# Selective scan with two states of a half in one scan instruction, and softplus from ScalarE's logarithm

## The chip, the cores and the metric

The kernel runs on one core of one Trainium2 chip. The metric is the device time of one execution in microseconds (us), taken as the median of several runs. The engines are named as the profile names them: PE is TensorE's matmul (PEld its weight load), DVE is VectorE, ACT is ScalarE, POOL is GpSimd, and SP is the engine that issues the plain DMAs. [...]

## What is computed

One layer adds two branches to its input. `x` is (2, 2048, 256) and is layer-normalized first. All data is float32.

```python
xn = _layernorm(x)
x  = x + attn(xn) + ffn(xn)

# attn: tokens sorted by the nearest of 8 means, then a Mamba scan along the sorted row
x_dbl = einsum('bdl,cd->bcl', u, x_proj_weight)          # u = sorted xn, transposed: (2, 256, 2048)
dts, Bm, Cm = x_dbl[:, :32], x_dbl[:, 32:48], x_dbl[:, 48:] + prompt
delta = softplus(einsum('brl,dr->bdl', dts, dt_projs_weight) + dt_projs_bias)
A = -exp(A_logs)                                           # (256, 16)
def step(h, (u_t, d_t, b_t, c_t)):                         # h: (2, 256, 16), along 2048 steps
    h = exp(d_t[..., None] * A) * h + (d_t * u_t)[..., None] * b_t[:, None, :]
    return h, einsum('bdn,bn->bd', h, c_t)
y = scan(step) + Ds * u                                    # then back to the old token order

# ffn: top 2 of 8 experts by w_gate, each silu(x w1) * (x w3), then w2
```

So there are 2 batches x 256 channels x 16 states = 8192 recurrences of 2048 steps each, and a mixture of experts with hidden width 512 over 4096 tokens.

## The kernel before

**The scan.** The sorted rows are cut into 8 *pieces* (2 batches x 4 stretches of CH = 512 tokens). In a piece the 256 channels are two *halves* `h` of 128 partitions, and the 16 states are NQ = 4 quarters of Q = 4 states. A *step* is one quarter of one half of one piece, so there are 64 steps, and each has 4 *places*, one for each state. At a place DVE multiplies `bu = du * B` (`feed`, L766) and runs one `tensor_tensor_scan` over 512 tokens with `da` and `bu` (`scan`, L775). ACT has made `da = exp(delta * A)` (`decay`, L760) one step ahead. The last column of each scan is kept in `carry` by a small ACT copy (`keep_last`, L781), and the same step of the next piece gives it to its scan as the start value.

The four scans of a step write interleaved into one tile `hs` (three buffers). At the places of the *next* step PE transposes `hs` in blocks (`turn`, L787, into two PSUM buffers `pt_s`), ACT copies each block to `ht` (L791), and PE multiplies `ht` with the masked C rows `z` into the sum `y` (`contract`, L796).

**Preparing a piece**, during the piece before: gather the rows, transpose them (`u`), project (`px`, then `xd`), write B and C to DRAM, load B rows back broadcast to all partitions (`load_b`, L680, tile `bt`, 1 MB for a quarter, two buffers) and C rows (`load_z`, L668), and compute the step size. `step_size` (L685 to L698) puts one matmul `pd` in PSUM and takes `|v|`, `relu(v)` and `exp(-|v|)` of it on ACT, for one half. Softplus is then `relu(v) + log(1 + e)`. The logarithm is a product of four quadratic factors: for each half four squares on ACT (`square`, L702) and four multiplies, one multiply-add and the product `du = delta * u` on DVE (`series`, L706 to L722). Each operation works on 512 columns.

**The mixture of experts.** 71 tiles of 128 token slots; each is three jobs: `part_up` twice (16 matmul instructions each into `p_ps`, L875, after a transpose `pt_g`, L858, copied to `xT`, L860) and `part_down` (`py`, L898). ACT does the tanh (L883) and scales the result (`yo`, L902), DVE does two multiplies (L888, L892). POOL fetches weights and rows and adds the results in DRAM by indirect DMAs. The matmul results `pd`, `px`, `pt_u`, `pt_g` and `py` share one pair of PSUM buffers (tag `m`), so the third one of these waits until ACT has read the first.

**The order.** It is written out. The loop from L1076 goes over the steps and their places and emits feed, scan, decay, turns and contract. `plan` holds the piece preparation by place (`at_place`). Into this the expert jobs are dealt so that PE's estimated work keeps a fixed ratio to DVE's estimated work (`ratio`, L1073), until `n_places`, 16 places before the end, after which all that remain are emitted at once. A last loop ties each engine's instructions to the order of the text, so no scheduler changes it.

Of the kernel before, what the change touches and what calls it, by code (L numbers as in the profile page):

```python
# [54 lines left out]
LOG1P = (  # L56
    (1.0093577, 1.1060627), (-0.08225194, 3.2574694), (-1.424736, 2.702104), (-2.321687, 0.43240654),
)
LOG1P_C = 0.0052326876


@with_exitstack
def scan_moe_kernel(
# [25 lines left out]
    JC = CH // P  # L89
    XP = R + 2 * NS  # L90
# [111 lines left out]
    log1p_a = cst.tile([P, len(LOG1P)], F32, name="log1p_a")  # L202
    for i, (a, _) in enumerate(LOG1P):
        nc.vector.memset(log1p_a[:, i : i + 1], a)
# [421 lines left out]
    class Piece:  # L626
# [51 lines left out]
        def load_b(self, q: int):  # L678
            bt = scn.tile([P, Q, CH], F32, tag="b", name="bt")
            nc.sync.dma_start(  # L680
                bt, bc_d[self.b][self.c][q * Q : (q + 1) * Q, :].partition_broadcast(P)
            )
            self.bts[q] = bt

        def step_size(self, h: int):  # L685

            if h == 0:
                self.e = pre.tile([P, ND, CH], F32, tag="tok", name="e")
                self.r = pre.tile([P, ND, CH], F32, tag="tok", name="r")
                self.sq = {}  # L690
# [7 lines left out]
            nc.scalar.activation(self.e[:, h, :], self.e[:, h, :], AF.Exp, scale=-1.0)  # L698

        def square(self, h: int, i: int):  # L700
            self.sq[h, i] = scn.tile([P, CH], F32, tag="sq", name="sq", bufs=3)
            nc.scalar.activation(  # L702
                self.sq[h, i], self.e[:, h, :], AF.Square, bias=log1p_a[:, i : i + 1]
            )

        def series(self, h: int, i: int):  # L706

            if h == 0 and i == 0:
                self.dl = prep.tile([P, ND, CH], F32, tag="dl", name="dl")
                self.du = prep.tile([P, ND, CH], F32, tag="du", name="du")  # L710
            dl = self.dl[:, h, :]
            if i < len(LOG1P):
                nc.vector.scalar_tensor_tensor(
                    dl, self.sq.pop((h, i)), LOG1P[i][1], dl if i else self.e[:, h, :],
                    ALU.add, ALU.mult,
                )
            elif i == len(LOG1P):
                nc.vector.scalar_tensor_tensor(
                    dl, dl, LOG1P_C, self.r[:, h, :], ALU.mult, ALU.add
                )  # L720
            else:
                nc.vector.tensor_mul(self.du[:, h, :], dl, self.u[:, h, :])  # L722
# [25 lines left out]
    carry = cst.tile([P, NQ, ND, Q], F32, name="carry")  # L748

    class Step:  # L750


        def __init__(self, piece: Piece, q: int, h: int):
            self.piece, self.q, self.h = piece, q, h
            self.da, self.bu, self.ht = [None] * Q, [None] * Q, [None] * JC

        def decay(self, i: int):
            n = self.q * Q + i
            self.da[i] = scn.tile([P, CH], F32, tag="da", name="da", bufs=6)
            nc.scalar.activation(  # L760
                self.da[i], self.piece.dl[:, self.h, :], AF.Exp, scale=na[:, self.h, n : n + 1]
            )

        def feed(self, i: int):
            self.bu[i] = scn.tile([P, CH], F32, tag="bu", name="bu", bufs=3)
            nc.vector.tensor_mul(  # L766
                self.bu[i], self.piece.du[:, self.h, :], self.piece.bts[self.q][:, i, :]
            )

        def scan(self, i: int):  # L770
            p, q, h = self.piece, self.q, self.h
            if i == 0:
                self.hs = late.tile([P, CH, Q], F32, tag="hs", name="hs", bufs=3)
            start = carry[:, q, h, i : i + 1] if p.c else 0.0
# [394 lines left out]
```

## Time and profile before

| | |
|---|---|
| median of 3 runs | 800.16 us (799.86 to 808.87) |
| the profiled execution, its own time | 793.45 us |
| its span, first to last instruction | 791.7 us |
| mean granted TensorE clock | 0.951 |
| PE instructions, DVE, ACT, POOL | 6552, 1162, 986, 374 |
| DMA, mean over the span | 159 GB/s, 61215 packets |

The span has three stretches. Up to about 115 us is the front: layer norm, choosing, sorting, and the preparation of the first piece. From 117 us, the first scan, to about 751 us scan and experts run side by side. From there to the end only the last scan places, their turns and the final additions run. The rows below are groups of instructions: line, engine, operation, tile, shapes and count, then busy time and mean ns of one, then the idle time of the engine just before them.

```profile
L875 PE MATMUL p_ps<-xT,w 128*128 128x128 f32 x2272 | 280.3, 279 | 5.3 <-ACT sq L702 4.3
L760 ACT ACTIVATE da<-dl,na 128x512 f32<-128x512 f32 x256 | 182.0, 723 | 1.1 <-DVE hs L775 1.0
L787 PE MATMUL pt_s<-ident,hs 128*128 128x128 f32 x1024 | 137.9, 279 | 14.7 <-ACT ht L791 8.7
L791 ACT COPY ht<-pt_s 128x512 f32<-128x512 f32 x256 | 137.1, 590 | 31.3 <-PE pt_s L787 31.0
```

### The profile page before, as it was taken

The numbers are of one execution on the slowest core, as the hardware profiler recorded it, in microseconds if no ns is written. First come the engines' busy times: TensorE is split into PE (matmuls) and PEld (weight loads), VectorE is DVE, ScalarE is ACT, GpSimd is POOL, SyncE is SP. The second block draws the span as 40 slices with busy tenths as digits, with TensorE's granted clock in tenths as the row PEclk, the third lists the DMA queues.
The fourth block names the chain that finished last, engine by engine and source line by source line (L and its number), as shares of the span: only waits on it lengthen the run. The fifth ranks groups of instructions, "written<-read, shape, count | busy, mean of one in ns | idle before, by whom it ended". The sixth has DMA issues, their size and how long they took to land.

```text
span 791.7 us, 16967 instructions
## 1 busy us (share of the span) xinstructions
PE 712.9 (90%) x6552; PEld 605.5 (76%) x6552; DVE 711.3 (90%) x1162; ACT 507.9 (64%) x986; POOL 520.9 (66%) x374
## 2 busy tenths in 40 slices
PE   7385979899999999899999999999999998999963
PEld 5144768589877988599868986798779885998842
DVE  8865269899999999899989999899999998899991
ACT  4821266586669657776668666866687576757572
POOL 2023738657867886788776787878678787686313
PEclk9755999999999999999999999999999998999996
DMA  8593244664368547855656367448644855444462
GB/s 280 222 323 114 58 173 108 210 172 97 108 155 244 154 106 215 203 148 143 206 140 176 56 247 219 107 95 263 197 111 132 273 156 112 107 102 96 86 219 27
DMA packets 61215, 125.90 MB, mean 159 GB/s; under 512 B 24464, under 2 KB 42032, under 8 KB 53776
## 3 DMA queue, kind: packets, MB, share of 16 engines
q0 software_dynamic: 40224, 65.03, 34.6%
q1 hardware_dynamic: 20912, 59.80, 22.1%
q8 instruction: 52, 0.85, 0.4%
q14 instruction: 27, 0.22, 0.1%
HBM read 180.06 MB, written 27.00 MB: 262 GB/s over the span
## 4 chain that ended last, share of the span: by engine, by line
PE 69%; ACT 6%; DVE 3%; issue 3%; DMA 2%; POOL 1%; POOLq 0%; SPq 0%; ACTq 0%; DVEq 0%
PE p_ps L875 28%; PE py L898 14%; PE pt_s L787 12%; PE y L796 6%; ACT ht L791 2%; DMA out_dram<-acc 2%; PE y L728 2%; PE pt_g L858 2%; PE px L655 2%; PE pd L692 1%; DVE hs L775 1%; ACT da L760 1%; DVE bu L766 1%; PE px L660 1%; PE pt_u L641 1%
## 5 line engine op out<-in xcount | busy, mean ns | idle before, releaser
L875 PE MATMUL p_ps<-xT,w 128*128 128x128 f32 x2272 | 280.3, 279 | 5.3 <-ACT sq L702 4.3
L875 PEld LDWEIGHTS p_ps<-xT,w 128*128 128x128 f32 x2272 | 268.2, 195 | 20.2 <-issue 9.3
L775 DVE TENSOR_TENSOR_SCAN hs<-da,carry,bu 128x512 f32<-128x512 f32 x192 | 246.2, 1283 | 0.0
L760 ACT ACTIVATE da<-dl,na 128x512 f32<-128x512 f32 x256 | 182.0, 723 | 1.1 <-DVE hs L775 1.0
L816 POOL DMA_INDIRECT acc<-yo,token_of x71 | 137.8, 1941 | 60.3 <-ACT yo L902 20.0
L766 DVE TENSOR_TENSOR bu<-du,bt 128x512 f32<-128x512 f32 x256 | 174.0, 680 | 0.0
L791 ACT COPY ht<-pt_s 128x512 f32<-128x512 f32 x256 | 137.1, 590 | 31.3 <-PE pt_s L787 31.0
L787 PE MATMUL pt_s<-ident,hs 128*128 128x128 f32 x1024 | 137.9, 279 | 14.7 <-ACT ht L791 8.7
L835 POOL DMA_INDIRECT w<-in_w_up_dram,w_row x71 | 94.8, 1335 | 84.2 <-DVE w_row L584 36.8
L898 PE MATMUL py<-w,g 128*128 128x256 f32 x568 | 139.0, 389 | 12.2 <-ACT r L696 8.7
L787 PEld LDWEIGHTS pt_s<-ident,hs 128*128 128x128 f32 x1024 | 117.7, 143 | 31.6 <-ACT ht L791 15.6
L898 PEld LDWEIGHTS py<-w,g 128*128 128x128 f32 x568 | 104.2, 193 | 27.1 <-ACT r L696 10.3
L849 POOL DMA_INDIRECT xg_sb<-xn,token_of x71 | 88.3, 1243 | 37.5 <-issue 30.2
L835 POOL DMA_INDIRECT w<-in_w_down_dram,w_row x71 | 93.5, 1317 | 21.6 <-issue 12.5
L883 ACT ACTIVATE t_sb<-p_ps 128x512 f32<-128x512 f32 x71 | 42.5, 599 | 69.4 <-PE p_ps L875 69.1
L902 ACT ACTIVATE yo<-py,own 128x256 f32<-128x256 f32 x71 | 33.8, 476 | 80.5 <-PE py L898 80.3
L775 DVE TENSOR_TENSOR_SCAN hs<-da,bu 128x512 f32<-128x512 f32 x64 | 78.2, 1223 | 0.0
L796 PE MATMUL y<-ht,z 128*32 128x128 f32 x2048 | 74.3, 279 | 2.5 <-ACT ht L791 1.9
L816 POOL DMA_INDIRECT acc<-yt,line_of x28 | 54.7, 1952 | 25.7 <-ACT ht L791 8.2
L796 PEld LDWEIGHTS y<-ht,z 128*32 128x32 f32 x2048 | 51.1, 110 | 24.5 <-issue 13.2
L888 DVE SCALAR_TENSOR_TENSOR t_sb<-t_sb,p_ps 128x512 f32<-128x512 f32 x71 | 48.2, 679 | 9.1 <-ACT t_sb L883 8.8
L892 DVE SCALAR_TENSOR_TENSOR g<-t_sb,p_ps 128x512 f32<-128x512 f32 x71 | 48.3, 681 | 7.2 <-PE p_ps L875 4.7
(188 smaller groups left out, 632.8 us busy)
## 6 DMA issues: line engine op xcount, KB each, us to landing
bt<-bc SPq DMA_DIRECT2D x32, 1024.0 KB, 5.4
z<-bc SPq DMA_DIRECT2D x32, 256.0 KB, 3.8
xn<-xt SPq DMA_DIRECT2D x8, 520.0 KB, 2.6
xt<-in_x_dram SPq DMA_DIRECT2D x8, 512.0 KB, 7.5
acc<-in_x_dram SPq DMA_DIRECT2D x8, 512.0 KB, 6.4
w<-in_w_up_dram,w_row POOLq DMA_INDIRECT x71
w<-in_w_down_dram,w_row POOLq DMA_INDIRECT x71
xg_sb<-xn,token_of POOLq DMA_INDIRECT x71
```

The source lines that it names most:

```text
L760: nc.scalar.activation(self.da[i], self.piece.dl[:, self.h, :], AF.Exp, scale=na[:, self.h, n : n + 1])
L766: nc.vector.tensor_mul(self.bu[i], self.piece.du[:, self.h, :], self.piece.bts[self.q][:, i, :])
L775: nc.vector.tensor_tensor_scan(self.hs[:, :, i], self.da[i], self.bu[i], start, ALU.mult, ALU.add)
L787: nc.tensor.transpose(pt[:, j, :], self.hs[:, t0 : t0 + G, :].rearrange("p t n -> p (t n)"), ident)
L791: nc.scalar.copy(self.ht[i], pt)
L796: nc.tensor.matmul(p.ys[self.h][j * G : (j + 1) * G, i, :], lhsT=p.zs[q][:, i * (P // G) + j, :], rhs=self.ht[i][:, j, :], start=False, st ...
L816: ins = nc.gpsimd.indirect_dma_start(out=to, out_offset=bass.IndirectOffsetOnAxis(ap=numbers, axis=0), in_=rows, in_offset=None, compute_o ...
L835: nc.gpsimd.indirect_dma_start(out=to[self.t % NW], out_offset=None, in_=rows, in_offset=bass.IndirectOffsetOnAxis(ap=w_row[:, self.t : se ...
L849: nc.gpsimd.indirect_dma_start(out=self.xg, out_offset=None, in_=xn_d, in_offset=bass.IndirectOffsetOnAxis(ap=token_of[:, self.t : self.t ...
L875: nc.tensor.matmul(p[:, f, :], lhsT=wk[:, h, f * P : (f + 1) * P], rhs=self.xT[:, h, :], start=h == 0, stop=h == ND - 1,)
L892: nc.vector.scalar_tensor_tensor(self.g, self.s, 0.5, self.p3, ALU.mult, ALU.mult)
L898: nc.tensor.matmul(py, lhsT=self.g[:, f, :], rhs=w2[:, f, :], start=f == 0, stop=f == NH - 1)
```

## The change

**Scan.** A step becomes 8 states of a half (32 steps, N_STEP = 8 places each; the number of places stays 256). One scan instruction covers two states: a tile of 2 x 513 columns, the states one after the other, each with an extra column in front. In that column `da` is 0 (set once), `du` is 1 and `bt` holds the carried value, so that the recurrence starts anew there. `feed` multiplies both states at once. The carried values are put into `bt` by a small ACT copy, `Step.begin`, two for each step. `da` lies in three fixed tiles, written 4 places ahead, `bu` has two buffers (before three), `hs` has two of twice the size (before three). `bt` is now loaded as two DMAs with rows of 2 KB, 3 places before `Step.begin` first touches it. The last step has 8 turns after its last scan, not 4.

**Softplus.** `exp(-|v|)` is taken for both halves in one ACT instruction, then `w = 1 + e`, then `Ln`. DVE adds `relu(v)` and what the rounding of `1 + e` lost. The squares and the product of factors are gone. In the built program the table load of ACT stands once before (L378), and 17 times after: for each piece one before the `Ln` and one before the next `Exp` or `Tanh`.

```diff
         def load_b(self, q: int):
-            bt = scn.tile([P, Q, CH], F32, tag="b", name="bt")
-            nc.sync.dma_start(
-                bt, bc_d[self.b][self.c][q * Q : (q + 1) * Q, :].partition_broadcast(P)
-            )
+            bt = scn.tile([P, 2, 2, CH1], F32, tag="b", name="bt")
+            r0 = q // 2 * 2 * Q + q % 2 * 2
+            for o in range(2):
+                rows = bc_d[self.b][self.c][r0 + o : r0 + o + Q + 1 : Q, :]
+                nc.sync.dma_start(bt[:, o, :, 1:], rows.partition_broadcast(P))
...
-            nc.scalar.activation(self.e[:, h, :], self.e[:, h, :], AF.Exp, scale=-1.0)
-
-        def square(self, h: int, i: int):
-            self.sq[h, i] = scn.tile([P, CH], F32, tag="sq", name="sq", bufs=3)
-            nc.scalar.activation(
-                self.sq[h, i], self.e[:, h, :], AF.Square, bias=log1p_a[:, i : i + 1]
-            )
+        def decay_of_one(self):
+            nc.scalar.activation(self.e, self.e, AF.Exp, scale=-1.0)
+            self.w = scn.tile([P, ND, CH], F32, tag="w", name="w", bufs=1)
+            nc.scalar.activation(self.w, self.e, AF.Identity, bias=ones[:, 0:1])
+
+        def log(self):
+            self.dl = prep.tile([P, ND, CH], F32, tag="dl", name="dl")
+            nc.scalar.activation(self.dl, self.w, AF.Ln)
+
+        def series(self, i: int):
+            if i == 0:
+                nc.vector.scalar_tensor_tensor(
+                    self.e, self.w, 1.0, self.e, ALU.subtract, ALU.subtract
+                )
+            elif i == 1:
+                nc.vector.tensor_sub(self.r, self.r, self.e)
+            elif i == 2:
+                nc.vector.tensor_add(self.dl, self.dl, self.r)
+            else:
+                self.du = prep.tile([P, ND, CH1], F32, tag="du", name="du")
+                nc.vector.memset(self.du[:, :, 0:1], 1.0)
+                nc.vector.tensor_mul(self.du[:, :, 1:], self.dl, self.u)
...
+        def begin(self, i: int):
+            p = self.piece
+            nc.scalar.copy(
+                p.bts[2 * self.s + i][:, :, :, 0],
+                carry[:, self.s, self.h, 2 * i : 2 * i + 2, :] if p.c
+                else zero[:, 0:4].rearrange("p (o n) -> p o n", n=2),
+            )
...
+        def feed(self, o: int):
+            self.bu[o] = scn.tile([P, 2, CH1], F32, tag="bu", name="bu", bufs=2)
             nc.vector.tensor_mul(
-                self.bu[i], self.piece.du[:, self.h, :], self.piece.bts[self.q][:, i, :]
-            )
+                self.bu[o], self.piece.du[:, self.h, :].unsqueeze(1).to_broadcast([P, 2, CH1]),
+                self.piece.bts[2 * self.s + o // 2][:, o % 2],
+            )
+
+        def scan(self, o: int):
+            if o == 0:
+                self.hs = late.tile([P, 2, CH1, Q], F32, tag="hs", name="hs", bufs=2)
             nc.vector.tensor_tensor_scan(
-                self.hs[:, :, i], self.da[i], self.bu[i], start, ALU.mult, ALU.add
+                self.hs.rearrange("p n t o -> p (n t) o")[:, :, o],
+                self.da[o].rearrange("p n t -> p (n t)"), self.bu[o].rearrange("p n t -> p (n t)"),
+                0.0, ALU.mult, ALU.add,
             )
...
-                for i, place in enumerate(((17, 18, 20, 21, 23, 25), (19, 22, 24, 26, 28, 30))[h]):
-                    if i < len(LOG1P):
-                        at_place(s1, place - 2, lambda p=p, h=h, i=i: p.square(h, i))
-                    at_place(s1, place, lambda p=p, h=h, i=i: p.series(h, i), 0.0, 0.6)
+            at_place(s1, 17, p.decay_of_one)
+            at_place(s1, 19, p.log)
+            for i, place in enumerate((19, 20, 22, 24)):
+                at_place(s1, place, lambda p=p, i=i: p.series(i), 0.0, 1.1)
...
+        if step:
+            if i % 2 == 0:
+                step.scan(i // 2)
+            elif i // 2 + 1 < Q:
+                step.feed(i // 2 + 1)
+            elif after_:
+                after_.feed(0)
+            if i == 1:
+                step.begin(1)
+            if after_ and i == 5:
+                after_.begin(0)
+            if i + AHEAD < N_STEP:
+                step.decay(i + AHEAD)
+            elif after_:
+                after_.decay(i + AHEAD - N_STEP)
+        if before_:
+            if i == 0:
+                before_.keep_last()
+            elif i in (1, 2, 4, 5):
+                for j in range(2):
+                    before_.turn(i // 4, (i - 1) % 3 * 2 + j)
+            elif i in (3, 6):
+                before_.contract(i // 4)
```

Loads of B in `plan`, in places of a piece of 32: before, quarter q at the step 2q - 3 (8 places before its first feed); after, at places 10 and 14 for the second half of the states and at 26 and 30 of the piece before for the first half. The same number of expert jobs is dealt, with DVE's estimates changed to (2.1, 1.1) for scan and feed.

## The prediction

> **What bounds the kernel now.** I read the engine totals and the chain that ended last first, then the waits and the stretches of 50 us, and last the timelines of PE and DVE.
>
> ```profile
> PE 712.9 (90%) x6552; PEld 605.5 (76%) x6552; DVE 711.3 (90%) x1162; ACT 507.9 (64%) x986; POOL 520.9 (66%) x374
> PE 69%; ACT 6%; DVE 3%; issue 3%; DMA 2%; POOL 1%; POOLq 0%; SPq 0%; ACTq 0%; DVEq 0%
> ```
>
> PE and DVE are equally busy, but the chain runs 69% over PE and 3% over DVE. The stretches say why:
>
> ```profile
> 250.00:300.00 50.00, 49.22 (x505) 45.63 (x504) 48.61 (x72) 34.69 (x70) 41.25 (x28) 1.00 0.54 145
> 300.00:350.00 50.00, 46.87 (x419) 39.39 (x419) 46.41 (x68) 37.49 (x74) 38.02 (x25) 0.97 0.77 215
> 331.00:335.00 4.00, 3.78 (x11) 3.03 (x12) 3.08 (x4) 1.29 (x4) 3.61 (x2) 0.58 0.85 259
> ```
>
> The columns after the length are busy PE, PEld, DVE, ACT, POOL, then PE's clock. PE is busy for 49.2 of 50 us in a good stretch. Adding up the idle time ahead of matmuls along PE's timeline from 115 to 752 us gives 21 us in 637, of which 20 stand against ACT (8.1 the copy `ht`, 7.7 the activation `r`, 3 others) and 0.4 against DVE. Nothing on PE's side waits for DVE there, so DVE's 97% is a coincidence of the dealing: DVE keeps pace with PE, it doesn't set it. Only from about 751 us, when the experts are done, do the last scans set the pace. Two of PE's waits are large:
>
> ```profile
> 331.22 3.40 PE L898 MATMUL py<-w,g 128*128 128x256 f32 x8 [3.13 <-ACT r L696]
> 667.99 3.78 PE L898 MATMUL py<-w,g 128*128 128x256 f32 x8 [3.13 <-ACT r L696]
> ```
>
> `py` needs a PSUM buffer that `pd` held until ACT had read it, and ACT came to that late, behind exponentials, squares and decays. The eight matmuls then took 3.40 and 3.78 us, where they take 1.99 elsewhere.
>
> **What DVE saves.** In the tail DVE runs alone:
>
> ```profile
> 758.37 0.67 DVE L766 TENSOR_TENSOR bu<-du,bt 128x512 f32<-128x512 f32 x1
> 758.95 1.28 DVE L775 TENSOR_TENSOR_SCAN hs<-da,carry,bu 128x512 f32<-128x512 f32 x1
> ...
> 760.14 0.67 DVE L766 TENSOR_TENSOR bu<-du,bt 128x512 f32<-128x512 f32 x1
> ```
>
> A place starts every 1.778 us (1.77 here; feed 0.58, scan 1.20), less than the sum of the durations, since instructions overlap. I take one column as 1.042 ns for a product and twice that for a scan (estimates; 512 columns are then 0.533 and 1.067 us, which leaves 0.05 and 0.13 us fixed). Two states of 1026 columns then cost 1.12 + 2.24 = 3.36 us instead of 3.556: 0.2 us for each of 128 pairs, 25 us in all. Softplus: 12 operations of about 0.60 us a piece become 4 of 1.12 and a small set: 2.6 us a piece, 21 us in all. Together 46 us, 6.5% of DVE's busy time. In the middle that is worth about nothing, because PE's work is unchanged (the same transposes, contractions and experts) and PE doesn't wait for DVE. If PE were not full, it would be worth up to 40 us.
>
> **The front.** The first softplus stands before the first scan. Before, the expert multiply (L888) that PE waited for started at 108.70, behind six operations. Now it stands behind two of 1.1 us that start after `Exp` and `1 + e`, near 105.4: about 107.7. PE gains 1 us (DVE some 2.5, not on the path).
>
> **The middle, what goes.** ACT's stretch ahead of `r` loses an `Exp` and up to two squares (0.6 us each, 1.8 together). In the built program's order `py` follows closely on `pd` in five of the seven later pieces. From ACT's queue I get PE waits of 0.9 (three times), 1.0 and 2.4, sum 6.1, against 7.7 now. The slow clock also goes: 1.4 + 0.3 us at 331 and 1.8 + 0.7 at 668 (`py` and the next transposes against 1.99 and 1.04), 4.2 us. The Trainium skill, "TensorE: Matmul & The Clock Gate", section "What's actually happening", has the clock halve after one idle window of about 3.4 us. Here it fell to 0.58 after 3.13 us, so I use the row; both leave 2.4 us unpunished, though with little room. Sum -5.8.
>
> **The middle, what comes: the logarithm on ACT.** For each piece ACT now has `Exp` 1.07, `1 + e` 1.17 and `Ln` 1.07 (from L698's 632 ns and L702's 734 for 512 columns; 256 more cost 219 between `xT`'s 380 and `u`'s 599) and two table loads.
>
> ```profile
> L378 ACT ACT_TABLE_LOAD x1 | 1.3, 1283 | 0.7 <-PEq L1158 0.7
> L702 ACT ACTIVATE sq<-e,log1p_a 128x512 f32<-128x512 f32 x64 | 46.4, 734 | 1.8 <-DVE dl L713 1.8
> L698 ACT ACTIVATE e<-e 128x512 f32<-128x512 f32 x16 | 10.1, 632 | 0.0
> L781 ACT COPY carry<-hs 128x4 f32<-128x4 f32 x48 | 8.7, 182 | 0.0
> ```
>
> In total ACT changes little: -46.4 - 10.1 + 8 x 3.3 + 16 x 1.283 + 64 `begin` copies at 0.18 (11.5) - 24 of the 48 carry copies (4.4) = -2 us of 508. But it comes in two blocks, 2.2 us at place 17 and 3.6 us at place 19 (load, `Ln`, load), and behind them queue the copies `ht` and `xT` that PE needs. I laid ACT's and PE's order side by side for three pieces with these durations. Because an expert job of 1.95 us mostly lies between a copy and its use, PE lost 0.6, 0.6 and 1.9 us; I take 1.0 x 7 = +7 us. Bounds: 0 (fully covered), and 3.5 x 7 = 25 us where nothing covers it. The skill speaks against this change: "ScalarE: Activation LUTs", section "Table sets: the hidden batching unit", would group activations by table set and counts some 2.7 us for each load with its drain. By that the load block is 2.8 us longer, PE would lose most of it, and the middle gets 15 to 20 us more. The row says 1.283 us, and its idle 0.7 stood at the program's start, so I keep the row and put the rule in the range.
>
> **The B rows.** They come in rows of 2 KB (512 of them to a megabyte, before 128), and the lead shrinks from 8 places to 3 before `begin`, a copy in ACT's own queue: where a load is late, decays, `ht` and tanh stand behind it, then PE. SP's queue is in order too: one of the loads stands behind the `bc` store, which waits for ACT's `xd`.
>
> ```profile
> bt<-bc SPq DMA_DIRECT2D x32, 1024.0 KB, 5.4
> z<-bc SPq DMA_DIRECT2D x32, 256.0 KB, 3.8
> bc<-xd SPq DMA_DIRECT2D x8, 64.0 KB, 2.2
> ```
>
> No row has 1 MB in 2 KB rows. At best it lands in 5.4 us as now. At worst it scales like `z`, which has such rows: 3.8 + 3 x 2.1 (1.6 us for 192 KB, so 2.1 for 256) = 10.2. I take 7.5. A place lasts (751 - 117)/240 = 2.6 us, three of them 7.9, and DVE, which frees the buffer, now has time to run ahead. So it is mostly hidden; for late ones in the busiest stretches (the longest landing now is 9.6) I put +2.
>
> **Other waits.** `hs` with two buffers lets PE lag three places behind DVE, and the multiply after each tanh already ties them to two. The three `da` tiles let ACT lead as before. Cost 0; their cover is DVE's new slack. If DVE gets none, each wait is a few us in all.
>
> **The tail.** 16 places run at DVE's pace: -16 x (1.778 - 1.68) = -1.6. After the last scan PE has 8 turns and two contractions instead of 4 and one. Now the last scan ends at 775.6 and the copy of the sum starts at 779.5; two further pairs of turns and a contraction at that rate add 2 x 1.2 + 1.2 = +3.6. Sum +2.
>
> **Sum.** -1 - 5.8 + 7 + 2 + 2 = +4.2 us on the profiled execution's 793.45, so 797.6. That execution lies 6.7 us below the median of the runs, so I expect 804 and put it at 803, as the waits that I priced don't all add.
>
> **Rivals.**
> - *PE's waits go* (14%). With slack on DVE and a thinner ACT queue at `r`, PE waits almost nowhere: -21 - 4.2 of the middle and -1, with +2 in the tail: 24 us less, 776. For it: 20 of 21 us stand against ACT. Against: ACT's total doesn't fall, and `ht` waits (8.1 us) come from two turns without a job between, which stay.
> - *Late B rows* (14%), the one on the other side. ACT stands at `begin` until `bt` has landed. PE has about 1 us of other work, so from a landing of 8.9 us (7.9 + 1) each further 0.1 costs 3 us over 30 loads. At 9.5 us it is +18: 821; at 10.2, +39. Against: DVE ahead by a place makes it harmless.
> - *The ACT block stops PE* (10%). 3.5 us each and the clock down: (3.5 + 1.9) x 7 = 38 instead of 7, so 834; half of that, 818.
> - *DVE isn't relieved*, because 1026 columns cost more than twice 512: DVE stays at 97%, PE still sets the pace, 803 to 808. It lies in my main case.
>
> **Numbers.** The main case (62%) is 803, 793 to 814. With a seventh on the fast side and a quarter on the slow side the range of 8 in 10 is 788 to 824. Two per cent, about what a measurement of this kernel can tell from no change, is 784 and 816. Faster: most of the first rival, 0.13. Slower: most of the second and third, 0.20. The rest 0.67.
>
> **What would show it.** DVE busy near 665 us with the same PE busy; scans near 2.3 us, feeds near 1.2; 17 table loads at 1.28; PE's idle between 115 and 752 still some 20 us, against ACT, and now at `ht` or `xT` behind `Ln`, with no granted clock near 0.5 in the middle; `bt` landing below 8 us and no long ACT wait for it. I'd be wrong if PE waited for DVE before, which its timeline denies, if ACT's rows for `begin` show waits on DMA, or if PE's busy time itself falls.

## The result, and the profile after

The change makes the kernel slower: 847.8 us against 804.28 us for the kernel before, both medians of four runs (846.17 to 848.95, and 799.86 to 808.87). The ratio is 1.0539, with a 95% interval of 1.0456 to 1.0622. The prediction said 803 us with a range of 788 to 824.

The two profiles differ by more than these medians. The profile of before is of an execution of 793.45 us, faster than all four runs above. That kernel takes 793.55 to 806.65 us on different chips (next section), and the changed kernel's profile (846.96 us) shows waits without a named releaser as only the slower chips have them. So some 10 us of the 53.5 between the two profiles may be the chip's.

First the engine totals and the chain that ended last, of the changed kernel. In the chain, the share of PE was 69% before.

```profile
PE 728.7 (86%) x6552; PEld 607.4 (72%) x6552; DVE 674.0 (80%) x849; ACT 510.0 (60%) x986; POOL 577.3 (68%) x374
PE 51%; DMA 13%; ACT 11%; issue 9%; POOL 8%; DVE 7%; POOLq 0%; SPq 0%; ACTq 0%; DVEq 0%
```

DVE is relieved by 37 us, as intended, and ACT's total hardly moves. But POOL, which executes none of the changed instructions, became 56 us busier with the same 374 instructions. The chain now runs over DMA and POOL, which had 3% between them.

Next the groups of instructions by line (busy us and mean ns of one, then the idle time before them):

```profile
L784 DVE TENSOR_TENSOR_SCAN hs<-da,bu 128x1026 f32<-128x1026 f32 x128 | 294.0, 2297 | 11.2 <-ACT da L769 1.9
L776 DVE TENSOR_TENSOR bu<-du,bt 128x1026 f32<-128x1026 f32 x128 | 156.3, 1221 | 19.5 <-ACT bt L756 15.7
L849 POOL DMA_INDIRECT w<-in_w_down_dram,w_row x71 | 111.7, 1573 | 21.6 <-issue 15.8
L830 POOL DMA_INDIRECT acc<-yt,line_of x28 | 68.8, 2456 | 24.4 <-ACT ht L804 11.9
L912 PE MATMUL py<-w,g 128*128 128x256 f32 x568 | 145.8, 402 | 30.8 <-DMA w<-in_w_down_dram,w_row 19.2
```

The same groups of the kernel before, for POOL:

```profile
L835 POOL DMA_INDIRECT w<-in_w_down_dram,w_row x71 | 93.5, 1317 | 21.6 <-issue 12.5
L816 POOL DMA_INDIRECT acc<-yt,line_of x28 | 54.7, 1952 | 25.7 <-ACT ht L791 8.2
```

POOL's fetch of the second weight took 1317 ns and now takes 1573 ns (that of the first 1335 and 1407), an addition of rows 1952 and now 2456. The `py` matmuls, which use those weights, have 19.2 us of new waiting for a DMA. The list of waits of the changed kernel (total us, times, longest us) says what PE waits for; before, neither weight load was in that list at all:

```profile
PE py L912 <- DMA w<-in_w_down_dram,w_row: 19.2, 7, 8.4
PE pt_s L800 <- ACT ht L804: 14.6, 19, 1.6
PE py L912 <- ACT r L691: 7.0, 6, 2.0
PE p_ps L889 <- DMA w<-in_w_up_dram,w_row: 5.3, 3, 2.7
```

Where do the 53.5 us between the two spans (791.7 and 845.2) lie? Up to the first scan +2.1 us, from the first scan to the end of the last expert job +48.2, behind that +3.2. (The kernel before with nothing changed but the rows of B, on one of the slower chips and no slower there, needs 643.7 us for that middle part instead of 634.1.) In the middle PE's idle time went from 21.4 to 58.6 us (+37.2) and its busy time for the same matmuls from 612.6 to 623.7 (+11.1): the first matmuls after a standstill are slow again. Added up along PE's timeline from 115 to 810 us, the idle time is 60.5 us: 24.5 against weight DMAs, 14.7 against the copy `ht`, 6.5 against `r`, 4.4 `xT`, 3.0 `u`, and 7.4 of the rest.

This is how a late weight comes about, in the timeline of the changed kernel (start us, duration us):

```profile
509.97 1.23 DVE L776 TENSOR_TENSOR bu<-du,bt 128x1026 f32<-128x1026 f32 x1 [1.32 <-ACT bt L756]
510.25 1.86 POOL L849 DMA_INDIRECT w<-in_w_down_dram,w_row  x1 [0.30 <-PE pt_s L800]
511.30 2.30 DVE L784 TENSOR_TENSOR_SCAN hs<-da,bu 128x1026 f32<-128x1026 f32 x1
512.42 1.98 POOL L849 DMA_INDIRECT w<-in_w_up_dram,w_row  x1 [0.31 <-PE pt_s L800]
514.70 0.97 POOL L863 DMA_INDIRECT xg_sb<-xn,token_of  x1 [0.30 <-issue]
514.98 3.45 PE L889 MATMUL p_ps<-xT,w 128*128 128x128 f32 x16 [2.75 <-DMA w<-in_w_up_dram,w_row]
```

POOL's fetch started at 512.42, in the middle of a scan that ended at 513.60, and ended at 514.40, 0.80 us after the scan. The next fetch met an idle DVE and took 0.97. Averaged over all of POOL's gathers from 115 us on that began while a scan was running, a fetch took 1479 ns before (88 of them) and 2053 ns after (82); those that met an idle DVE took 1.14 and 1.08 us. Of 75 gathers of the changed kernel that began with over 0.6 us of a scan still to run, four fifths ended between 0.76 and 0.85 us after that scan's end, and before the median of 61 such gathers was 0.80 us too: what they wait for is the end of the scan. Not every DVE instruction does this. The 33 gathers that began during the multiplies L902 and L906, one of whose two inputs lies in PSUM, took 0.99 us.

POOL had no room for that. The stretch from 500 to 550 us, before and then after (columns as in the prediction):

```profile
500.00:550.00 50.00, 48.20 (x468) 44.47 (x467) 48.90 (x78) 35.08 (x72) 40.16 (x30) 1.00 0.60 160
```

```profile
500.00:550.00 50.00, 43.08 (x348) 34.15 (x348) 36.50 (x38) 31.93 (x61) 39.99 (x23) 0.93 0.64 144
```

Between two of its instructions POOL stands at least 0.30 us (often "issue" in its timeline). Before, 30 instructions of 40.16 us and 30 such pauses made 49.2 of 50 us: POOL was full there, and its 66% of the span hid it. (From 117 to 751 us it is 476.9 us in 315 instructions, with their pauses 571 of 634 us, 90%.) After, the same busy time carries 23 instructions, and PE falls from 48.2 to 43.1 us.

DVE's own gain is smaller than its busy time says. Its timeline where it runs alone, in the tail of the changed kernel:

```profile
806.24 1.20 DVE L776 TENSOR_TENSOR bu<-du,bt 128x1026 f32<-128x1026 f32 x1
807.55 2.30 DVE L784 TENSOR_TENSOR_SCAN hs<-da,bu 128x1026 f32<-128x1026 f32 x1
809.76 1.20 DVE L776 TENSOR_TENSOR bu<-du,bt 128x1026 f32<-128x1026 f32 x1
```

A pair of states starts every 3.52 us; two places of the kernel before took 2 x 1.778 = 3.56. Merging two scans into one gains 0.04 us, not 0.2: before, each instruction began before the one ahead had ended; now there is a gap of 0.11 us behind each feed (806.24 + 1.20 to 807.55), which isn't counted as busy.

The gap comes with the order. Before, the loop feeds one place ahead, so that a scan never follows the feed whose output it reads, and all 255 scans that follow a feed directly begin about 0.08 us before its end. The change emits each feed right before its scan, and at 81 of the 82 places where the two stand side by side DVE idles 0.10 us or more, while behind a long scan the next feed still begins 0.09 us early. The length of the instructions isn't the reason: in the last kernel of the fifth group below both feed and scan are split, so that no scan follows the feed of its own input, and its pairs start every 3.44 us without a gap:

```profile
769.66 1.27 DVE L778 TENSOR_TENSOR bu<-du,bt 128x513 f32<-128x513 f32 x2
770.85 2.34 DVE L787 TENSOR_TENSOR_SCAN hs<-da,bu 128x513 f32<-128x513 f32 x2
773.10 1.27 DVE L778 TENSOR_TENSOR bu<-du,bt 128x513 f32<-128x513 f32 x2
```

A joined pair with the feed one place further ahead would take about 3.33 us (an estimate: 3.52 less the gap of 0.10 and an overlap of 0.09 in its place). No run shows that.

### The profile page after: what moved, and what is told of

Its sections match the earlier page's. It is cut to its first block, busy times and chain, and to the rows that moved or that the text cites. A ratio compares the mean times of both kernels' runs of the same rounds, so it can differ in the third digit from the quotient of the medians.

```text
span 845.2 us, 16770 instructions
## 1 busy us (share of the span) xinstructions
PE 728.7 (86%) x6552; PEld 607.4 (72%) x6552; DVE 674.0 (80%) x849; ACT 510.0 (60%) x986; POOL 577.3 (68%) x374
## 4 chain that ended last, share of the span: by engine, by line
PE 51%; DMA 13%; ACT 11%; issue 9%; POOL 8%; DVE 7%; POOLq 0%; SPq 0%; ACTq 0%; DVEq 0%
PE p_ps L889 20%; PE py L912 10%; PE pt_s L800 7%; PE y L810 4%; POOL acc L830 4%; DMA w<-in_w_up_dram,w_row 4%; DMA w<-in_w_down_dram,w_row 4%; ACT ht L804 3%; POOL w L849 2%; ACT da L769 2%; DMA out_dram<-acc 2%; PE px L649 2%; PE pd L687 2%; PE pl L331 1%; DVE st L363 1%
## 5 line engine op out<-in xcount | busy, mean ns | idle before, releaser
L784 DVE TENSOR_TENSOR_SCAN hs<-da,bu 128x1026 f32<-128x1026 f32 x128 | 294.0, 2297 | 11.2 <-ACT da L769 1.9
L830 POOL DMA_INDIRECT acc<-yo,token_of x71 | 141.0, 1985 | 68.8 <-ACT da L769 11.5
L912 PE MATMUL py<-w,g 128*128 128x256 f32 x568 | 145.8, 402 | 30.8 <-DMA w<-in_w_down_dram,w_row 19.2
L776 DVE TENSOR_TENSOR bu<-du,bt 128x1026 f32<-128x1026 f32 x128 | 156.3, 1221 | 19.5 <-ACT bt L756 15.7
L849 POOL DMA_INDIRECT w<-in_w_up_dram,w_row x71 | 99.9, 1407 | 74.4 <-DVE w_row L578 36.2
L912 PEld LDWEIGHTS py<-w,g 128*128 128x128 f32 x568 | 107.4, 199 | 49.6 <-issue 14.2
L849 POOL DMA_INDIRECT w<-in_w_down_dram,w_row x71 | 111.7, 1573 | 21.6 <-issue 15.8
L863 POOL DMA_INDIRECT xg_sb<-xn,token_of x71 | 100.5, 1416 | 37.9 <-issue 17.4
L830 POOL DMA_INDIRECT acc<-yt,line_of x28 | 68.8, 2456 | 24.4 <-ACT ht L804 11.9
L902 DVE SCALAR_TENSOR_TENSOR t_sb<-t_sb,p_ps 128x512 f32<-128x512 f32 x71 | 48.5, 683 | 43.3 <-ACT t_sb L897 34.7
L906 DVE SCALAR_TENSOR_TENSOR g<-t_sb,p_ps 128x512 f32<-128x512 f32 x71 | 48.4, 681 | 14.5 <-PE p_ps L889 8.9
L874 ACT COPY xT<-pt_g 128x256 f32<-128x256 f32 x71 | 26.8, 378 | 40.1 <-PE pt_g L872 40.0
```

The lines of the kernel that those rows point to most:

```text
L776: nc.vector.tensor_mul(self.bu[o], self.piece.du[:, self.h, :].unsqueeze(1).to_broadcast([P, 2, CH1]), self.piece.bts[2 * self.s + o // 2] ...
L784: nc.vector.tensor_tensor_scan(self.hs.rearrange("p n t o -> p (n t) o")[:, :, o], self.da[o].rearrange("p n t -> p (n t)"), self.bu[o].re ...
L830: ins = nc.gpsimd.indirect_dma_start(out=to, out_offset=bass.IndirectOffsetOnAxis(ap=numbers, axis=0), in_=rows, in_offset=None, compute_o ...
L849: nc.gpsimd.indirect_dma_start(out=to[self.t % NW], out_offset=None, in_=rows, in_offset=bass.IndirectOffsetOnAxis(ap=w_row[:, self.t : se ...
L863: nc.gpsimd.indirect_dma_start(out=self.xg, out_offset=None, in_=xn_d, in_offset=bass.IndirectOffsetOnAxis(ap=token_of[:, self.t : self.t ...
L902: nc.vector.scalar_tensor_tensor(self.s, self.s, 1.0, self.p1, ALU.add, ALU.mult)
```

## The experiments

The kernels ran on five chips, here called A to E; the kernel before took 804.47 us on A, 793.55 on B, 802.75 on C, 806.65 on D and 795.50 on E. Each ratio is to the kernel before on the same chip. The table is of chip A; its last columns are from each kernel's trace: POOL's busy time, and PE's waits for weights from 115 to 810 us. The row of the change is the result above, from a series of its own, whose kernel before took 804.28 us. On the faster chips B and E the change itself was not run.

| kernel | us | ratio (95%) | POOL | PE for weights |
|---|---|---|---|---|
| the change | 847.8 | 1.0539 (1.0456 to 1.0622) | 577.3 | 24.5 |
| scan split | 829.14 | 1.0302 (1.0232 to 1.0372) | 504.6 | 3.1 |
| rows of B at 8 KB | 836.59 | 1.0404 (1.0348 to 1.0460) | 568.7 | 10.7 |
| before, new softplus | 814.11 | 1.0112 (1.0066 to 1.0157) | 514.5 | 0 |
| change, old softplus | 857.03 | 1.0624 (1.0563 to 1.0684) | 584.6 | 13.5 |

**First group: one part of the change undone, or done alone.** The scan is split, with all else as in the change:

```diff
-            nc.vector.tensor_tensor_scan(
-                self.hs.rearrange("p n t o -> p (n t) o")[:, :, o],
-                self.da[o].rearrange("p n t -> p (n t)"), self.bu[o].rearrange("p n t -> p (n t)"),
-                0.0, ALU.mult, ALU.add,
-            )
+            for n in range(2):
+                nc.vector.tensor_tensor_scan(
+                    self.hs[:, n, :, o], self.da[o][:, n, :], self.bu[o][:, n, :],
+                    0.0, ALU.mult, ALU.add,
+                )
```

> The changed kernel, but each scan of 1026 columns is issued as two scans of 513; products, B rows, softplus and order stay as changed. Theory 1 (a DVE instruction of 2.3 us keeps POOL's DMA issues waiting about twice as long, POOL's queue falls behind and expert weights land late): POOL busy falls from 577 to about 530 us, PE's waits for weights from 27 to under 8 us, and the time from 848 to 805-822. Theory 2 (B rows in 2 KB pieces slow the transfers): POOL and weights stay, time 845-860, since DVE only gets longer. Theory 3 (the logarithm's block on ACT): 845-860.

Measured 829.14 us. Its engine totals, and POOL's weight fetch:

```profile
PE 726.1 (88%) x6552; PEld 608.1 (73%) x6552; DVE 680.2 (82%) x977; ACT 509.2 (61%) x986; POOL 504.6 (61%) x374
L849 POOL DMA_INDIRECT w<-in_w_down_dram,w_row x71 | 93.9, 1323 | 21.6 <-issue 14.9 <-PE pt_s L800 3.7 <-PE p_ps L889 1.5
```

DVE's busy time rises by 6 us with 128 more instructions, POOL's falls by 73 without any edit to POOL; a fetch is back at 1323 ns, one that meets a scan at 1350 ns, and PE's waits for weights are gone but for 3.1 us. In this case that is the direct evidence that the length of a DVE instruction holds POOL up. But a remainder of 3% stays, more than the first theory expected (805 to 822 us).

The rows of B come back to 8 KB. The first column of a row is then loaded as well, and the projection's rows are ordered so that four states lie next to each other:

```diff
-            r0 = q // 2 * 2 * Q + q % 2 * 2
-            for o in range(2):
-                rows = bc_d[self.b][self.c][r0 + o : r0 + o + Q + 1 : Q, :]
-                nc.sync.dma_start(bt[:, o, :, 1:], rows.partition_broadcast(P))
+            rows = bc_d[self.b][self.c][q * Q : (q + 1) * Q, :]
+            nc.sync.dma_start(
+                bt.rearrange("p o n t -> p (o n) t"), rows.partition_broadcast(P)
+            )
...
```

> The changed kernel, but B is stored with its extra column and in the order of use, so that a load of B is again one piece of 8 KB for each partition (one DMA for a quarter). Theory 1: POOL stays near 577 us, waits for weights stay above 20 us, time 838-850. Theory 2: waits for weights fall under 8 us, time 805-822. Theory 3: 840-850.

Measured 836.59: part of the loss. POOL stays slow (568.7), but PE's waits for weights halve (10.7 us), which neither theory expected. How short rows delay weights isn't shown. It isn't by slower transfers: from the first to the last packet of a first weight (1 MB in rows of 8 KB, some 22 of them) pass 3.88 us in the median with the short rows of B and 4.01 with the long ones.

The new softplus alone, in the kernel before (scan, step and rows as before; its methods are those of the change, and only the placing is shown):

```diff
-                for i, place in enumerate(((17, 18, 20, 21, 23, 25), (19, 22, 24, 26, 28, 30))[h]):
-                    if i < len(LOG1P):
-                        at_place(s1, place - 2, lambda p=p, h=h, i=i: p.square(h, i))
-                    at_place(s1, place, lambda p=p, h=h, i=i: p.series(h, i), 0.0, 0.6)
+            at_place(s1, 17, p.decay_of_one)
+            at_place(s1, 19, p.log)
+            for i, place in enumerate((19, 20, 22, 24)):
+                at_place(s1, place, lambda p=p, i=i: p.series(i), 0.0, 1.1)
```

> The kernel before with the softplus part of the change alone (Exp, 1 + e and Ln for both halves, 17 table loads, at the changed places). Theory 1: POOL stays near 525 us (few long DVE instructions are added), weights arrive in time, 795-812. Theory 2: 795-812 too. Theory 3: most of the loss is here, 825-850, with PE waits for copies behind the Ln.

And the reverse of it, the changed scan with the old softplus:

> The changed kernel with the softplus of before (squares on ACT, product of factors on DVE in 512 columns). Theory 1: POOL stays near 570 us, waits for weights stay above 20 us, 838-860. Theory 2: the same. Theory 3: 800-820.

The new softplus costs the kernel before 1.1% on this chip, but with the long scan the old one is dearer still, 1.0624 against 1.0539. So the larger part of the loss comes with the scan, not with the logarithm.

**Second group: are rows and scan two costs or one?** Four kernels on chip D: the change unaltered, with each of the two edits, and with both.

> The change unaltered, as the corner of four kernels on one chip: one scan of 1026 columns or two of 513, and the B rows in 2 KB or in 8 KB. Both theories: 1.045 to 1.062 of the time before, with PE waiting some 25 us for weights and POOL busy near 577 us.

> Only the scan is split, rows stay at 2 KB. If POOL, held up by the long scan, is the main cost: at least 1.8% below the unaltered change on this chip, POOL near 505 us, waits for weights below 5 us. If the rows are the main cost: within 1% of it.

> Only the rows of B are 8 KB, the scan stays whole. If rows cost by themselves: 1.3% below the unaltered change or more, as on the earlier chip. If they only cost because POOL is late: about as much (0.5 to 1.3%), with POOL still near 570 us and a wait for weights of 8 to 15 us left.

> Both. If rows cost by themselves: 1% below the split scan with 2 KB rows. If rows cost only through POOL: the same as the split scan within 0.5%. Either way something of 1.5 to 3.5% above the kernel before should be left that neither explains; if it is below 1%, the two causes explain all and the earlier rest was the chip's.

| | 2 KB rows | 8 KB rows |
|---|---|---|
| one scan of 1026 | 1.0500 (1.0391 to 1.0609), POOL 565.2, weights 14.3 | 1.0280 (1.0166 to 1.0393), POOL 572.6, weights 9.7 |
| two scans of 513 | 1.0427 (1.0341 to 1.0513), POOL 507.8, weights 2.7 | 1.0295 (1.0198 to 1.0392), POOL 507.2, weights 1.5 |

The effect on POOL repeats (a fetch that meets a scan: 1985 and 2028 ns whole, 1379 and 1384 split), and so does that on the waits. The effect on the time doesn't repeat so well. Both edits together return about 2 of 5%, but here the rows alone return as much, and the split alone 0.7%, against more than 2% between the two ratios of the first group. The intervals here are 1% to either side, so how the 2% divides between scan and rows stays open. The split scan was expected to return at least 1.8% here if POOL were the main cost, and didn't: that long scans slow POOL and delay weights is shown in both groups; that time is lost by it only in the first (2.4 of 5.4%, against 0.7 of 5.0% here, within the noise).

Something that isn't in the profile of before stopped the split scan of this group, and may have hidden some of its gain. Its stretch from 660.80 to 665.90 us, and then the first instructions behind it:

```profile
660.80:665.90 5.10, 0.00 (x0) 0.00 (x0) 0.02 (x1) 1.09 (x3) 3.59 (x3) 0.94 0.77 236
```

```profile
665.95 0.69 DVE L906 SCALAR_TENSOR_TENSOR g<-t_sb,p_ps 128x512 f32<-128x512 f32 x1 [5.13 <-remote]
665.99 0.37 ACT L874 COPY xT<-pt_g 128x256 f32<-128x256 f32 x1 [4.10 <-remote]
666.41 3.78 PE L889 MATMUL p_ps<-xT,w 128*128 128x128 f32 x16 [5.62 <-issue]
```

PE, DVE and ACT stand together and resume within half a microsecond, and the profile names no releaser. Such waits of ACT and DVE ("issue" or "remote"), added up from 117 to 780 us, make 32.5 us here, 21.0, 17.4 and 15.0 in the other three of this group, and 15.5 in the change's own profile. They come with the chip: on A, C and D every kernel has 6.6 to 32.5 us of them, the kernel before with the new softplus 19.5 and with short rows 10.1; the seven kernels run on B and E have none, and neither has the profile of before. The kernel before itself is 7 to 13 us slower on A, C and D than on B and E. What causes them the runs don't show.

**Third group: the short rows in the kernel before**, on chip C.

```diff
-            bt = scn.tile([P, Q, CH], F32, tag="b", name="bt")
-            nc.sync.dma_start(
-                bt, bc_d[self.b][self.c][q * Q : (q + 1) * Q, :].partition_broadcast(P)
-            )
+            bt = scn.tile([P, 2, 2, CH + 1], F32, tag="b", name="bt")
+            for o in range(2):
+                rows = bc_d[self.b][self.c][q * Q + o : q * Q + o + 3 : 2, :]
+                nc.sync.dma_start(bt[:, o, :, 1:], rows.partition_broadcast(P))
...
```

> The kernel before with only the B loads as in the change: two DMAs a quarter, rows of 2 KB at a pitch of 513 columns, still 8 places ahead. If the rows cost 1.1 to 1.3% by themselves, as between the kernels with and without them (1.054 to 1.040, 1.030 to 1.019): ratio 1.009 to 1.015. If they cost only with the change's short lead of 3 places or its late POOL: 0.998 to 1.004.

Measured 804.81 us, ratio 1.0007 (0.9981 to 1.0033). The profile counts 74017 packets instead of 61215, and they cost nothing where POOL keeps up and the loads have eight places of lead.

**Fourth group: what the logarithm costs.** The next kernel, on chip B, is the new softplus in the kernel before, with a square in place of the logarithm: the computation changes, but not the number or size of the instructions, and the 16 table loads fall away.

```diff
-            nc.scalar.activation(self.dl, self.w, AF.Ln)
+            nc.scalar.activation(self.dl, self.w, AF.Square)
```

> The kernel before with the softplus part, but Square, a function of the table already loaded, in place of Ln (the output is not the reference's): the same instructions without 16 table loads. If the loads cost the 10 us: 802-807. If it is the lump of three ACT instructions of 1024 columns: 811-815.

Measured 796.97, ratio 1.0044 (1.0032 to 1.0055), against 1.0073 (1.0047 to 1.0098) and 1.0112 with the loads on E and A. So the 16 loads of 1283 ns cost about 0.3 to 0.7%, 2 to 5 us (across chips, so roughly), and the block without them 0.4%, 3.4 us.

The same edit in the change with split scan and 8 KB rows, on chip C:

> Split scans and 8 KB rows, with Square in place of Ln (the output is not the reference's), so that the 16 table loads go and the ACT instructions stay. If the loads are most of the 1.9% that is left: ratio 1.004 to 1.012. If the order of work by steps of 8 is: 1.014 to 1.019.

It gave 829.94, ratio 1.0351 (1.0274 to 1.0428): no gain over the 1.0295 that the kernel with its loads had on chip D. Next to that, on chip C itself, the next kernel keeps its loads and stands at 1.0331. So the loads aren't the remainder. `Exp` and `1 + e` were taken by halves, two places apart, on chip C:

> Split scans and 8 KB rows, with Exp and 1 + e for each half by itself, at places 15 and 17, instead of both at 17 (four ACT instructions of 0.65 to 0.75 us instead of two of 1.1). If the long ACT instructions in one place keep PE's copies waiting: PE's waits for ht and xT fall by 3 us or more, ratio 1.012 to 1.016. If not, or if Relu is now late: 1.018 to 1.025.

Measured 830.12, ratio 1.0331 (1.0291 to 1.0371), against 1.0295 with whole blocks on chip D: nothing says that the block's size is the remainder either. Both kernels lie above all that was expected of them, since the expectations rested on chip B's 1.0187 (fifth group). The kernel with both edits alone was not run on C.

**Fifth group: what remains with both edits.** On chip B the kernel with both edits, and the split scan with the old softplus:

> The split scans and the B rows in 8 KB pieces together, all else as changed. If long scans (theory 1) and the 2 KB rows (theory 2) cost separately: 814-822, PE's waits for weights 0-2 us. If the rows only hurt where POOL is behind already: 825-832, no different from the split scans alone (829).

> The changed kernel with split scans and with the softplus of before: what is left of the change is the order of work by steps of 8 states, the extra column with its small copies, the 2 KB rows. If the logarithm costs 10 us here as it does on the kernel before: 817-823. If it is a saving here, as without the split scans (857 without it, 848 with it): 832-842.

809.50 (1.0187, 1.0148 to 1.0225) and 820.54 (1.0329, 1.0303 to 1.0354). These two differ in rows and softplus at once, so they don't part the two; POOL is busy 514.7 and 523.0 us in them, near the 520.9 of before. Then, on chip E, the new softplus alone, both edits, and both edits with the feed split into two of 513 columns as well:

```diff
-            nc.vector.tensor_mul(
-                self.bu[o], self.piece.du[:, self.h, :].unsqueeze(1).to_broadcast([P, 2, CH1]),
-                self.piece.bts[2 * self.s + o // 2][:, o % 2],
-            )
+            for n in range(2):
+                nc.vector.tensor_mul(
+                    self.bu[o][:, n, :], self.piece.du[:, self.h, :],
+                    self.piece.bts[2 * self.s + o // 2][:, o % 2, n, :],
+                )
```

> The kernel before with the new softplus alone, now beside the two kernels below on one chip, as the lower end of what the change must cost. Both theories: 1.007 to 1.016, since nothing in it lengthens a DVE instruction in the scan.

> The change with the scan split and the rows at 8 KB, on the same chip: 1.019 to 1.035, with POOL busy near 507 us. What it stands above the new softplus alone is the rest that neither the scan nor the rows explain.

> As the second, and the feed of 1026 columns is split into two of 513 as well, so that every DVE instruction of the scan has the length it had before. If the long feed makes up the rest (POOL and the copies behind it wait for it): 1% or more below the second, POOL a further 5 to 10 us less busy. If the rest lies in the coarser step of the work (four turns and two contractions come at once, and PE waits for their copies ht): within 0.5% of the second, and PE still waits 15 us or more for ht.

Measured 801.91 (1.0073, 1.0047 to 1.0098), 805.79 (1.0154, 1.0110 to 1.0197) and 808.87 (1.0186, 1.0124 to 1.0248). The long feed isn't the rest. Between the first two lie 0.8% by the ratios (0.5% by the medians), and PE's list of waits in the second shows no POOL and hardly a DMA:

```profile
PE pt_s L801 <- ACT ht L805: 15.1, 20, 1.6
PE py L913 <- ACT r L692: 7.0, 6, 2.0
PE p_ps L890 <- ACT yo L917: 4.4, 2, 3.3
```

With POOL free, the rows long and no standstills, what is left of the change costs 1.5%, half of it the logarithm's. That is less than the 1.9 to 3.5% that was expected. The other half is what the runs leave to the coarser step and its order, by exclusion only: I didn't try a step of four states with joined scans. The waits for `ht`, first in the list, don't decide it. From 115 us on they are 18.4 us, but 17.0 with the new softplus alone, whose step is the old one. What grew most between these two kernels is the wait for `r`, from 2.4 to 6.5 us, of 7.6 us more idle time in all; why ACT comes later to `r` in the new order isn't shown. The same structure stood at 1.03 on C and D, where there are standstills. How much of that difference is theirs, and why the kernel before loses less there, is open.

**Sixth group: is the kernel before held by `r`?** On chip B, `Exp` is moved out from ahead of `r` and taken once for both halves, with the old logarithm, whose squares now stand one place ahead of their use and not two:

```diff
-            nc.scalar.activation(self.e[:, h, :], self.e[:, h, :], AF.Exp, scale=-1.0)
+        def decay_of_one(self):
+            nc.scalar.activation(self.e, self.e, AF.Exp, scale=-1.0)
...
+                if h == 0:
+                    at_place(s1, 17, p.decay_of_one)
-                for i, place in enumerate(((17, 18, 20, 21, 23, 25), (19, 22, 24, 26, 28, 30))[h]):
+                for i, place in enumerate(((18, 19, 20, 21, 23, 25), (20, 22, 24, 26, 28, 30))[h]):
```

> The kernel before with the two Exp of a piece taken as one, at place 17, and the squares after it, so that ACT reads pd (Abs, Relu) sooner. If PE's two waits of 3.1 us at py and the slow clock after them are due to the Exp and squares ahead of Relu: these waits fall to about 1 us and the time to 793-800. If other ACT work takes their place: 802-808.

The longest wait for `r` fell from 3.13 to 1.40 us as expected, and the kernel was 2.4% slower, outside both ranges that were expected: 813.97, ratio 1.0236 (1.0191 to 1.0282). In its list of waits stand instead

```profile
PE p_ps L877 <- DVE g L894: 4.9, 6, 1.3
PE p_ps L877 <- ACT ht L793: 2.9, 3, 1.1
```

The wait for `g` was 0.4 us before. Of 11 us more idle time of PE 4.5 stand against `g` and 3.7 against `ht`. So DVE, at 97% in the middle, seems not free to take work at another place, although PE doesn't wait for it as dealt.

## Why the prediction was wrong

The step that failed is the one under **Other waits**: "Cost 0; their cover is DVE's new slack." Those waits were the tile buffers between DVE, ACT and PE, and POOL's queue was not among them. No term of the sum asked what a DVE instruction of twice the length does to an engine that has nothing to do with the scan. The page showed POOL at 520.9 us, 66%, which looks like room, and the prediction doesn't mention it; in the stretch shown above it was full. The trace puts 24.5 us of PE's idle time on weights that came late, where the sum had nothing, and with the split scan 3.1 were left. That step is shown; it isn't the whole loss. Scan and rows together returned 2 of the 5%, the logarithm costs about 1, and what remains is under *What remains*.

The Trainium skill, "SBUF — State Buffer", section "Who interferes with whom", states a mechanism: a DVE instruction with two inputs in SBUF contends with a GpSimd instruction that reads SBUF, and the ports that the two share are an exclusive lock. The same section infers that the issue of a DMA is spared by such instructions. Here the issue of an indirect DMA is not spared: fetches that began in a scan ended 0.8 us after it, and the mean fetch that met a scan moved with the scan's length, 1479, 2053 and 1350 ns for 512, 1026 and 513 columns. Which port it is, no run shows. The step could have been priced, as an estimate from the rows of before: a scan's added length is about 1 us, half of it is met on average, so 0.5 us for each fetch that meets a scan. The traces show 0.57.

Step by step:

- *What DVE saves*: the busy time fell by 37.3 us, where 46 were expected, but 0.2 us for a pair was wrong. The period fell by 0.04 us, 5 us over 128 pairs. The estimate took the feed and the scan of a pair as if nothing stood between them; the changed order puts each scan right behind the feed that it reads, and the gap and the lost overlap, 0.19 us a pair, are as much as joining was to save. Of what was gained 0.12 us a pair may be the start value that three quarters of the scans took before (1283 ns with it, 1223 without). That DVE's relief is worth about nothing held.
- *The middle, what goes*: PE's waits for `r` were put at 6.1 us and measured 6.5, none longer than 2.04. The slow clock didn't go. That 2.4 us of waiting go unpunished was wrong: after that wait of 2.04 us (at 258.27) the granted clock was 0.57 from 258 to 262 us and the eight `py` took 3.53 us, while two waits of 1.94 and 2.07 us for weights had no such effect. PE also found other waits, and the mean granted clock in the middle fell from 0.992 to 0.985. The 4.2 us were not gained. (The parts given for the waits of before, 8.1, 7.7 and 3, don't make 20; by the trace `ht` and `r` are 7.7 each and the others 4.5.)
- *The logarithm*: +7 us for PE's new waits on ACT. With the new softplus alone, on chip E, they are +6.0 for `ht` (13.7 against 7.7 up to 752 us) and +2.5 for `xT`, with `r` 5.3 less, and its whole cost is 0.7%, on chip A 1.1%. The size was about right, and the trace's 1.283 us for a load was the better number than the rule's 2.7: ACT stands 0.02 us ahead of a load and 0.01 behind it.
- *The B rows*: +2 us, for loads that ACT waits for. ACT waited for no `bt`: where DVE stood against the copy of the carried value (15.7 us), ACT had merely come to it late. Rows cost 1 to 2% beside the long scan and nothing in the kernel before, so the rival of late B rows named one right edit and the wrong way for it to act.
- *The front*: -1 was expected and +2.1 measured; there DVE waited once, 15.7 us, for `1 + e` (before: 13.8 us for a square). Over all kernels run here the first scan starts anywhere between 111.6 and 121.6 us, so neither number means much.
- *The tail*: +2 was expected, +3.2 measured. Up to the end of the last scan it was 2.0 us shorter, where 1.6 were expected, but not for the reason given: the period accounts for 0.3. Behind the last scan it was 5.2 us longer, where 3.6 were expected.
- *What remains* with both edits: 0.8% above the softplus on chip E, left to the coarser step by exclusion, and more on the chips with standstills without a named releaser. No term stood for either.

No version beat the kernel before.

## What to carry to other kernels

A longer instruction isn't only its own time: ask who starts work beside it and may have to wait until it ends, and price it for the queues off the path too, POOL's DMA issues first. Joining instructions can also join a producer to its reader: look at what stands directly behind what. Read an engine's room in the busiest stretch with its pauses counted, not from its share of the span. Work taken off an engine that doesn't set the pace buys nothing, and in an order that was dealt by hand even a wait that is truly removed can cost more than it was worth.

## What the runs showed of the hardware

A fetch that POOL issued while a scan ran took 1.35 to 1.57 us on average with scans of 512 or 513 columns (fifteen kernels), and 1.96 to 2.16 us with scans of 1026 (five kernels); one that began in a multiply with an input in PSUM took 0.99. POOL stands at least 0.30 us between two such instructions, and that isn't counted as busy. Two DVE instructions in a row overlap by about 0.08 us, but where the second reads what the first wrote, there is a gap instead, 0.10 us in the change; with that, joining saved 1% of a pair and not the 5.6% that was expected. On three of the chips ACT and DVE had 6.6 to 32.5 us of waits without a named releaser, on the other two none. And PE, after it had stood for 2.04 and for 8.38 us, took 3.53 and 3.71 us for eight `py` matmuls that take 1.99 elsewhere, so such a wait can cost over 1.5 us more than itself:

```profile
258.27 3.53 PE L912 MATMUL py<-w,g 128*128 128x256 f32 x8 [2.04 <-ACT r L691]
797.75 3.71 PE L912 MATMUL py<-w,g 128*128 128x256 f32 x8 [8.38 <-DMA w<-in_w_down_dram,w_row]
```
